# A gated cross-attention layer in f32: the down product of its feed-forward part by a 26-product scheme

## The chip, the core and the metric

The kernel runs on one core of a Trainium2 chip. A core has TensorE (PE: matrix products, out of the on-chip memory SBUF into the accumulators of PSUM), VectorE (DVE), ScalarE (ACT), GpSimd (POOL[...]) and SyncE (SP, which issues most DMA transfers). All data is f32. The metric is device time in microseconds of one execution, lower is better.

## What is computed

The input x has 64 sequences of 128 tokens with 512 features, the context ctx has the same shape. The reference, cut to what matters:

```python
x = x + tanh(g_xattn) * xattn(layernorm(x), ctx, ctx, ...)
# xattn: Q, K, V = per-head products with Wh; scores summed over the whole batch,
#        A = max(|sum_b scores * decay|, 1); O = A V; Y = norm(O) * gamma + beta
#        return (relu(x @ wg_w) * Y) @ wo_w
x = x + tanh(g_ffn) * ffn(layernorm(x), ...)
# ffn: g = (xf @ gate_w.T) * gate_s;  u = (xf @ up_w.T) * up_s
#      return ((silu(g) * u) @ down_w.T) * down_s
```

INTER, the hidden width of ffn, is 1408: 11 tiles of 128. The change concerns the last product, `(silu(g) * u) @ down_w.T`, called "down" below.

## The kernel before

The work goes in 16 groups of four sequences (512 tokens, four token tiles). A first pass over all groups normalises x, forms the scores and the gate projection, and stores what later stages need in DRAM; beside it, `prepare_weights` reads the raw weights, lets GpSimd form the sums of weight blocks that the fast schemes need, and stores them in DRAM scratch (`gu_scr`, `dn_scr`, `wo_scr`), one part per group, each part a load, its sums, and its stores one group later.

A second pass runs, for each group g, `ffn(g)`; beside it, for later groups, `attended(g+1)` (the product with wo, the residual, the second layer norm) and `next_retention(g+2)` (A V, the normalisation, the product with the gate). All three are Python generators. `interleave` draws from them in a fixed ratio: ffn has the weight FFN_STEPS, the attention chain int(23 x 1.05) = 24; the next step is drawn from the generator for which (steps done + 1) / weight is least. The order in which steps are drawn is the order of the program. From it a planner makes each engine's instruction order: by its own estimates of durations, a free engine is given, among the instructions whose operands are ready, the one that comes first in the program. An engine then runs its instructions strictly in that order, each waiting for its operands.

The big products use two-by-two schemes with seven block products in place of eight. Gate and up: `ffn` runs over five values of j; for each it takes the two INTER tiles j and 5 + j, and makes seven products of four matmuls (128x128 weights, 256 columns), each called by `product` (line 216). They accumulate in PSUM banks bank_a, bank_f, bank_b and two banks bank_c0 and bank_c1 that take turns. `hidden` (lines 783 and 784) makes silu(gate) on ScalarE and multiplies by up on VectorE. Two of the four blocks need an add out of PSUM first: c22 (line 813, out of bank_c) and c12 (line 818, out of bank_b). The order within one j is: bank_f, bank_a, bank_c (then a ScalarE copy bank_b <- bank_c, line 804), the first product of the next j into bank_a, bank_c (c22), bank_b (c12), bank_c again. The last of these waits until c22 has been read out of bank_c. After that GpSimd forms four sums of hidden blocks (lines 256 to 259, `combine_a`), the left-hand sides of down.

The eleventh INTER tile is the leftover: `rest_product` (line 850) computes it with the same scheme on half blocks, 14 matmuls in the midst of the down stage.

Down before: two halves of the tokens, two halves of INTER (five tiles each) and two halves of DIM. Each of the seven `down_product`s (line 836) has ten matmuls of 256 columns and fetches its own weights of 640 KB (line 767, three buffers); `down_rest` (line 893) adds the eleventh tile with eight matmuls. Six adds (line 902) bring 128x512 blocks out of PSUM into x_t, the residual, and two ScalarE copies (lines 880 and 913) carry a partial sum to another bank.

Beside it, VectorE does for the attention chain: the adds of the wo product (line 660), batch statistics (lines 180 and 181), normalisation (line 208) and a 32x32 block transpose (line 192) whose result goes through DRAM (`moved`, lines 198 and 201) and comes back token-transposed. In `retention` these follow for all four sequences in one step of the generator, the one after the fourth product `po` (line 571). `combine_tokens` (line 253) makes the four sums of the next group's tokens, on GpSimd after the first group; it reuses one buffer, so it starts after the last product that reads the present ones.

Of the kernel before, what the change touches and what calls it, by code (L numbers as in the profile page):

```python
# [10 lines left out]
F32 = mybir.dt.float32  # L11
# [15 lines left out]
DB11, DB21, DB22, DT1, DT2, DT3, DT4 = range(7)  # L27

# [28 lines left out]
def flamingo_gated_layer(  # L57
# [22 lines left out]
    P = 128  # L80
# [64 lines left out]
    dn_rest = const.tile([P, DIM], F32, name="dn_rest")  # L145
# [3 lines left out]
    dn_scr = dram.tile([7, P, NJ, HN], F32, name="dn_scr")  # L149
# [110 lines left out]


# [42 lines left out]
    decay = once.tile([P, H, S], F32, name="decay")  # L304
    ds = once.tile([P, DIM], F32, name="ds")
# [38 lines left out]
    def load_down(j):  # L344
        raw = once.tile([P, 2, DIM], F32, tag="raw", name="dn_raw", bufs=2)
        pair = downT[0 : REST * P].rearrange("(q j p) e -> p q j e", q=2, p=P)[:, :, j, :]
        nc.sync.dma_start(out=raw, in_=pair)
        return raw

    def sum_down(j, raw):  # L350

        for q in range(2):
            nc.gpsimd.tensor_tensor(raw[:, q], raw[:, q], ds, ALU.mult)
        t = once.tile([P, 4, HN], F32, tag="sums", name="dn_t")
        b = (raw[:, 0, 0:HN], raw[:, 0, HN:DIM], raw[:, 1, 0:HN], raw[:, 1, HN:DIM])
        combine_b(nc.gpsimd, [t[:, i] for i in range(4)], *b)
        return [
            (dn_scr[0, :, j], b[0]),
            (dn_scr[1:3, :, j].rearrange("m p e -> p m e"), raw[:, 1].rearrange("p (m e) -> p m e", m=2)),
            (dn_scr[3:7, :, j].rearrange("m p e -> p m e"), t),  # L360
        ]

    def load_down_rest():
        nc.sync.dma_start(out=dn_rest, in_=downT[REST * P : INTER])

    def sum_down_rest(_):
        nc.gpsimd.tensor_tensor(dn_rest, dn_rest, ds, ALU.mult)
        rest_weights()
        return []
# [20 lines left out]
    def prepare_weights():  # L390


        parts = [(load_wo, sum_wo)]
        for j in range(NJ):
            parts.append((partial(load_down, j), partial(sum_down, j)))
            parts.append((partial(load_gu, j), partial(sum_gu, j)))
        parts.append((load_down_rest, sum_down_rest))
        raw, stores = parts[0][0](), []
        yield
        for n, (_, sums) in enumerate(parts):  # L400
            for dst, src in stores:
                nc.sync.dma_start(out=dst, in_=src)
            stores = sums(raw)
            if n + 1 < len(parts):
                raw = parts[n + 1][0]()
            yield
        for dst, src in stores:
            nc.sync.dma_start(out=dst, in_=src)

# [27 lines left out]
    def scores(g, c_t, xnT):  # L437
# [10 lines left out]
        for h in range(H):  # L448
            if h % 2 == 0:
                tags = ("v", "sq") if g % 2 else ("ys", "yT")  # L450
                both = att.tile([P, 2, 2, 3, P], F32, tag=tags[h // 2], name="both")
# [183 lines left out]
    def attended(g, x_t, ws, x1nT):  # L635
# [4 lines left out]
        s = att.tile([P, 4, KC, HT], F32, tag="ys", name="ys")  # L640
# [97 lines left out]

    gup = ctx.enter_context(tc.tile_pool(name="gup", bufs=2))
    dnp = ctx.enter_context(tc.tile_pool(name="dnp", bufs=3))  # L740
    work = ctx.enter_context(tc.tile_pool(name="work", bufs=2))
    comb = ctx.enter_context(tc.tile_pool(name="comb", bufs=1))
    turn = [0]

# [20 lines left out]
    def down(m):  # L765
        w = dnp.tile([P, NJ, HN], F32, tag="dn", name="dn_w")
        nc.sync.dma_start(out=w, in_=dn_scr[m])
        return w

    def ffn(g, x_t, x1nT, tokens):  # L770

        b11, b21, b22, t = tokens
        h11 = comb.tile([P, NJ, HT], F32, tag="h11", name="h11")
        h21 = comb.tile([P, NJ, HT], F32, tag="h21", name="h21")
        h22 = comb.tile([P, NJ, HT], F32, tag="h22", name="h22")
        hs = comb.tile([P, 4, NJ, HT], F32, tag="hs", name="hs")
        hrest = comb.tile([P, TOK], F32, tag="hrest", name="hrest")

        def hidden(dst, src, i):

            n = dst.shape[-1]
            sil = work.tile([P, HT], F32, tag="sil", name="sil", bufs=3)
            nc.scalar.activation(sil, src[:, 0:n], AF.Silu, scale=gs_sb[:, i : i + 1])  # L783
            nc.vector.scalar_tensor_tensor(  # L784
                dst, src[:, n : 2 * n], us_sb[:, i : i + 1], sil, ALU.mult, ALU.mult
            )

        w = gu_next[0]
        product(bank_a, w[GA11], b11, True)
        yield  # L790
        for j in range(NJ):
            i1, i2 = j, NJ + j
            bank_c = next_c()
            m5 = work.tile([P, TOK], F32, tag="m5", name="m5")
            h12 = work.tile([P, HT], F32, tag="h12", name="h12")
            nc.scalar.copy(bank_c, bank_a)  # L796
            product(bank_f, w[GS1], t[:, 0], True)
            nc.scalar.copy(m5, bank_f)
            yield
            product(bank_a, w[GA12], b21, False)  # L800
            hidden(h11[:, j, :], bank_a, i1)
            yield
            product(bank_c, w[GS2], t[:, 1], False)
            nc.scalar.copy(bank_b, bank_c)  # L804
            yield
            w_j = w
            if j + 1 < NJ:
                w = gate_up(j + 1)
                product(bank_a, w[GA11], b11, True)
            yield  # L810
            product(bank_c, w_j[GS3], t[:, 2], False)
            c22 = work.tile([P, TOK], F32, tag="c", name="c22")
            nc.vector.tensor_add(c22, bank_c, m5)  # L813
            hidden(h22[:, j, :], c22, i2)
            yield
            product(bank_b, w_j[GS4], b22, False)
            c12 = work.tile([P, TOK], F32, tag="c", name="c12")
            nc.vector.tensor_add(c12, bank_b, m5)
            hidden(h12, c12, i1)
            yield  # L820
            product(bank_c, w_j[GA22], t[:, 3], False)
            hidden(h21[:, j, :], bank_c, i2)

            combine_a(
                nc.gpsimd, [hs[:, i, j, :] for i in range(4)],
                h11[:, j, :], h21[:, j, :], h12, h22[:, j, :],
            )
            yield
        if g + 1 < NG:
            gu_next[0] = gate_up(0)  # L830

        def down_product(bank, m, lhs, start):
            dn = down(m)
            for i in range(2):
                for j in range(NJ):
                    nc.tensor.matmul(  # L836
                        bank[:, i * HN : (i + 1) * HN],
                        lhsT=lhs[:, j, i * P : (i + 1) * P],
                        rhs=dn[:, j, :],
                        start=(start and i == 0 and j == 0),  # L840
                        stop=(i == 1 and j == NJ - 1),
                        skip_group_check=True,
                    )
                yield
# [10 lines left out]
        def rest_silu(gate):  # L855
            sil = work.tile([P, HT], F32, tag="sil", name="sil", bufs=3)
            nc.scalar.activation(sil, gate, AF.Silu, scale=gs_sb[:, REST:NI])
            return sil

        def rest_hidden(tok, sil, up):  # L860
            nc.vector.scalar_tensor_tensor(
                hrest[:, tok], up, us_sb[:, REST:NI], sil, ALU.mult, ALU.mult
            )

        half = slice(0, HT)
# [3 lines left out]
        nc.scalar.copy(bank_c[:, half], bank_a[:, half])  # L869
        rest_product(bank_f, GS1, t[:, 0], True)  # L870
        nc.scalar.copy(m5[:, half], bank_f[:, half])
        yield
        rest_product(bank_a, GA12, b21, False)
        sil = rest_silu(bank_a[:, half])
        rest_product(bank_c, GS2, t[:, 1], False)
        nc.scalar.copy(bank_b[:, half], bank_c[:, half])
        yield
        bank_d = next_c()
        yield from down_product(bank_f, DB11, h11, True)
        nc.scalar.copy(bank_d, bank_f)  # L880
        rest_product(bank_c, GS3, t[:, 2], False)
        c22 = work.tile([P, TOK], F32, tag="c", name="c22")
        nc.vector.tensor_add(c22[:, half], bank_c[:, half], m5[:, half])
        rest_product(bank_b, GS4, b22, False)
        c12 = work.tile([P, HT], F32, tag="h12", name="c12")
        nc.vector.tensor_add(c12, bank_b[:, half], m5[:, half])
        rest_product(bank_c, GA22, t[:, 3], False)
        rest_hidden(slice(HT, TOK), rest_silu(c12), c22[:, half])
        rest_hidden(half, sil, bank_c[:, half])
        yield  # L890
        def down_rest(bank, q, cols, stop=True):
            for i in range(2):
                nc.tensor.matmul(
                    bank[:, i * HN : (i + 1) * HN],
                    lhsT=hrest[:, (2 * q + i) * P : (2 * q + i + 1) * P],
                    rhs=dn_rest[:, cols],
                    start=False, stop=(stop and i == 1), skip_group_check=True,
                )

        def add(q, cols, bank):  # L900
            dst = x_t[q][:, :, cols]
            nc.vector.tensor_add(dst, dst, bank.rearrange("p (b d) -> p b d", b=2))
# [127 lines left out]
```

## Time and profile before

| | us |
|---|---|
| median of the runs | 2286.45 |
| the profiled execution, its own time | 2287.32 |
| its span, first to last instruction | 2285.5 |
| PE busy | 2264.5 |
| DVE busy | 901.0 |
| ACT busy | 601.4 |
| POOL busy | 670.1 |

The granted TensorE clock was 0.998 of full speed. 475.9 MB went over DMA, 208 GB/s as a mean; the queue of SP carried 457 MB of it.

A second-pass group takes 116.6 us (a product of the same place starts at 1121.10, 1237.67 and 1354.24 us). The first pass ends and the second begins near 400 us. In the stretch of gate and up of one group (1139 to 1215 us) PE was busy for 75.78 of 76 us, VectorE for 30.31, GpSimd for 20.03, and DMA 65% of the time; in the stretch of down (1215 to 1242 us) PE for all 27.00 us, VectorE 11.28, GpSimd 9.40, DMA 74%.

How to read the rows: "L836 PE MATMUL bank_f<-dn_w,h ... x640 | 143.5, 379" is the line of the kernel, the engine, the operation, what is written from what, the shapes, the number of records, their busy time in us and the mean of one in ns; what follows the second bar is the engine's idle time ahead of them and what ended it. A row of the timeline starts with the start and the duration in us; "x8" are eight records of one group in a row, and a bracket at its end is the idle time ahead of it and its releaser. One f32 matmul of the code leaves two records.

### The profile page before, as it was taken

The numbers are of one execution on the slowest core, as the hardware profiler recorded it, in microseconds if no ns is written. First come the engines' busy times: TensorE is split into PE (matmuls) and PEld (weight loads), VectorE is DVE, ScalarE is ACT, GpSimd is POOL, SyncE is SP. The second block draws the span as 40 slices with busy tenths as digits, with TensorE's granted clock in tenths as the row PEclk, the third lists the DMA queues.
The fourth block names the chain that finished last, engine by engine and source line by source line (L and its number), as shares of the span: only waits on it lengthen the run. The fifth ranks groups of instructions, "written<-read, shape, count | busy, mean of one in ns | idle before, by whom it ended". The sixth has DMA issues, their size and how long they took to land.

```text
span 2285.5 us, 27188 instructions
## 1 busy us (share of the span) xinstructions
PE 2264.5 (99%) x10304; PEld 1925.1 (84%) x10304; DVE 901.0 (39%) x1835; ACT 601.4 (26%) x1116; POOL 670.1 (29%) x811
## 2 busy tenths in 40 slices
PE   8999999999999999999999999999999999999999
PEld 6878887778888888888888888888888888888888
DVE  6544443654434343434343434333434333333222
ACT  3444444321212122212122222222221212121221
POOL 4222300232242424233323242424232323333210
PEclk9999999999999999999999999999999999999999
DMA  8787875766666665656565756666666656564541
GB/s 279 251 275 259 266 246 164 257 209 218 206 209 212 208 213 196 214 197 219 185 223 187 226 191 220 188 223 191 221 200 207 214 191 219 199 203 159 166 150 65
DMA packets 167794, 475.89 MB, mean 208 GB/s; under 512 B 16112, under 2 KB 52592, under 8 KB 150896
## 3 DMA queue, kind: packets, MB, share of 16 engines
q1 hardware_dynamic: 162240, 457.12, 61.2%
q10 hardware_dynamic: 5424, 17.04, 1.9%
q8 instruction: 81, 1.33, 0.2%
q14 instruction: 49, 0.40, 0.1%
HBM read 376.72 MB, written 97.39 MB: 207 GB/s over the span
## 4 chain that ended last, share of the span: by engine, by line
PE 93%; DVE 3%; DMA 1%; POOL 1%; issue 1%; SPq 0%; ACT 0%; ACTq 0%; DVEq 0%; POOLq 0%
PE bank_c L216 20%; PE bank_a L216 13%; PE bank_c L836 9%; PE bank_f L216 7%; PE bank_f L836 6%; PE bank_b L216 6%; PE sv L457 4%; PE by L649 3%; PE bank_b L836 3%; PE bank_a L836 3%; PE bz L649 2%; PE bx L649 2%; PE pq L442 2%; PE po L571 2%; PE bank_c L850 2%; PE bank_a L850 1%
## 5 line engine op out<-in xcount | busy, mean ns | idle before, releaser
L216 PE MATMUL bank_c<-tcomb,gu 128*128 128x256 f32 x1920 | 456.3, 380 | 3.7 <-DVE c L813 3.0
L216 PEld LDWEIGHTS bank_c<-tcomb,gu 128*128 128x128 f32 x1920 | 362.2, 190 | 72.2 <-ACT bank_b L804 10.1
L216 PE MATMUL bank_a<-x1nT,gu 128*128 128x256 f32 x1280 | 303.0, 379 | 0.7 <-ACT bank_c L796 0.7
L216 PEld LDWEIGHTS bank_a<-x1nT,gu 128*128 128x128 f32 x1280 | 242.8, 190 | 40.4 <-issue 6.2
L256 POOL TENSOR_TENSOR hs<-h,h 128x256 f32<-128x256 f32 x80 | 58.1, 727 | 649.8 <-DVE h L784 649.8
L176 POOL TENSOR_TENSOR rs<-ve,mhalf 128x1 f32<-128x1 f32 x128 | 73.5, 586 | 318.9 <-DVE ve L175 303.7
L783 ACT ACTIVATE sil<-c,gs_sb 128x256 f32<-128x256 f32 x160 | 81.2, 508 | 285.3 <-DVE c L813 184.8
L216 PE MATMUL bank_b<-x1nT,gu 128*128 128x256 f32 x640 | 151.6, 379 | 0.0
L216 PE MATMUL bank_f<-tcomb,gu 128*128 128x256 f32 x640 | 151.3, 379 | 0.0
L836 PE MATMUL bank_c<-dn_w,hs 128*128 128x256 f32 x640 | 145.0, 382 | 0.0
L813 DVE TENSOR_TENSOR c<-bank_c,m 128x512 f32<-128x512 f32 x80 | 54.7, 684 | 227.1 <-PE bank_c L216 223.7
L836 PE MATMUL bank_f<-dn_w,h 128*128 128x256 f32 x640 | 143.5, 379 | 0.0
L836 PEld LDWEIGHTS bank_c<-dn_w,hs 128*128 128x128 f32 x640 | 120.3, 190 | 19.8 <-ACT bank_b L913 4.0
L836 PEld LDWEIGHTS bank_f<-dn_w,h 128*128 128x128 f32 x640 | 121.6, 190 | 17.4 <-issue 1.0
L216 PEld LDWEIGHTS bank_b<-x1nT,gu 128*128 128x128 f32 x640 | 121.9, 190 | 16.7
L216 PEld LDWEIGHTS bank_f<-tcomb,gu 128*128 128x128 f32 x640 | 121.6, 190 | 16.5
L630 POOL TENSOR_TENSOR w_t<-w_t,yT 128x256 f32<-128x256 f32 x112 | 77.9, 727 | 159.7 <-ACT yT L621 159.7
L180 DVE BATCH_NORM_STATS2 st<-x_t 128x6 f32<-128x512 f32 x128 | 83.8, 682 | 94.0 <-DMA x_t<-in_x_dram 92.9
L457 PE MATMUL sv<-qw,c_t 128*128 128x256 f32 x512 | 120.4, 379 | 0.0
L784 DVE SCALAR_TENSOR_TENSOR h<-c,us_sb,sil 128x256 f32<-128x256 f32 x160 | 78.5, 491 | 84.3 <-ACT sil L783 84.3
L783 ACT ACTIVATE sil<-bank_a,gs_sb 128x256 f32<-128x256 f32 x80 | 37.9, 474 | 277.1 <-PE bank_a L216 277.1
L660 POOL TENSOR_TENSOR x_t<-x_t,m 128x512 f32<-128x512 f32 x48 | 60.8, 1296 | 168.3 <-ACT m L666 168.3
(166 smaller groups left out, 3484.4 us busy)
## 6 DMA issues: line engine op xcount, KB each, us to landing
gu<-gu_scr SPq DMA_DIRECT2D x80, 1024.0 KB, 4.9
dn_w<-dn_scr SPq DMA_DIRECT2D x112, 640.0 KB, 4.0
gu<-gu_scr SPq DMA_DIRECT2D x80, 768.0 KB, 4.8
x_t<-in_x_dram SPq DMA_DIRECT2D x62, 512.0 KB, 5.5
sq_scr<-sq SPq DMA_DIRECT2D x30, 1024.0 KB, 4.2
wo_w<-wo_scr SPq DMA_DIRECT2D x112, 256.0 KB, 2.7
c_t<-in_ctxT_dram SPq DMA_DIRECT2D x64, 256.0 KB, 4.9
v_scr<-both SPq DMA_DIRECT2D x32, 512.0 KB, 6.5
```

Of the source, the lines that this page charges most:

```text
L176: nc.gpsimd.tensor_tensor(dst, ve, mhalf[:, :n], ALU.pow)
L180: nc.vector.bn_stats(st, src)
L216: nc.tensor.matmul(out, lhsT=w[:, s, k, :], rhs=x_k, start=(start and s == 0 and k == 0), stop=(s == 1 and k == KC - 1), skip_group_check= ...
L256: engine.tensor_tensor(s[0], a21, a22, ALU.add)
L457: nc.tensor.matmul(sv[:, 0 : 2 + i : 1 + i, :], lhsT=c_t[j][:, h, :], rhs=qw[:, h, j : GB + 1 : GB - j, :], start=(i == 0), stop=(i == 1), ...
L630: (helper if d else nc.gpsimd).tensor_tensor(w, w, yT[:, :, d * KC + k, q * 2 : q * 2 + 2, :], ALU.mult)
L649: nc.tensor.matmul(bank[:, i * HN : (i + 1) * HN], lhsT=lhs[:, k, i * P : (i + 1) * P], rhs=w[:, k, :], start=(start and i == 0 and k == 0 ...
L660: engine.tensor_tensor(dst, dst, src.rearrange("p (b d) -> p b d", b=2), ALU.add)
L783: nc.scalar.activation(sil, src[:, 0:n], AF.Silu, scale=gs_sb[:, i : i + 1])
L784: nc.vector.scalar_tensor_tensor(dst, src[:, n : 2 * n], us_sb[:, i : i + 1], sil, ALU.mult, ALU.mult)
L836: nc.tensor.matmul(bank[:, i * HN : (i + 1) * HN], lhsT=lhs[:, j, i * P : (i + 1) * P], rhs=dn[:, j, :], start=(start and i == 0 and j == ...
L850: nc.tensor.matmul(out, lhsT=gu_rest[:, m, k, :], rhs=x_k, start=(start and k == 0), stop=(k == KC - 1), skip_group_check=True,)
```

## The change

Down becomes a scheme for four token tiles, four tiles of INTER and two halves of DIM: 26 products of 128x128 by 128x256 in place of 32. The eleven INTER tiles are dealt out as DOWN_QUADS: two quads (0, 1, 6, 5) and (2, 3, 8, 7), each with 26 products, and a triple (10, 9, 4), with which 20 of the 26 suffice. The quads and the triple share the order DOWN_STEPS: 24 steps, each with an accumulator, one or two products, each with up to three matmuls (one of either quad, one of the triple), and the blocks of x_t to which the accumulator is added or from which it is subtracted. An accumulator is not cleared between its steps: each add reads the running sum in place, and the signs in DOWN_STEPS are chosen for that. There are six accumulators of 256 columns: a, f, b0, b1, c0, c1, in five banks.

- The left-hand sides are sums of 128x128 hidden tiles, made in place in 26, 26 and 20 slots: 28 sums for each quad (H_SUMS), 18 for the triple (H_SUMS3). The first quad's are on GpSimd (18 at j = 2, 10 at j = 3), eight of the second's too (j = 3); its other 20 are on VectorE at j = 4. The triple's are on VectorE: eight after c12 of j = 4, ten after the last product.
- VectorE clears bank_b, half of bank_c1 and half of bank_c0 by memsets ahead of down.
- The leftover tile's gate and up products go first in the group.
- The first five steps ("roots") run with both quads first, then with the triple.
- The weights of one product are a tile of 128 x 3 x 256, two thirds of it where the triple is left out; nine buffers, the first nine fetched during gate and up, each further one after the product that frees its buffer.
- 28 adds of 128x256 go into x_t, in place of six of 128x512; the two copies are gone.
- In the preparation, the weight sums of down are made per quad: 8 products with the scale (three of them on VectorE) and 18 sums of 128x256 for a quad, 6 and 12 for the triple. `prepare_weights` takes all gate/up parts first, then the three of down.
- FFN_STEPS is 50 (it was 56). `both` takes turns in three buffers in place of four, `ys` shares the buffer of `sq`, `decay` and `ds` live in buffers of wo.

```diff
-    def down(m):
-        w = dnp.tile([P, NJ, HN], F32, tag="dn", name="dn_w")
-        nc.sync.dma_start(out=w, in_=dn_scr[m])
+    def down(n):
+        w = dnp.tile([P, 3, HN], F32, tag="dn", name="dn_w")
+        tiles = 3 if in_three[n] else 2
+        nc.sync.dma_start(out=w[:, 0:tiles], in_=dn_scr[weights_at[n], :, 0:tiles])
         return w
...
+        sums = {
+            2: [(nc.gpsimd, 0, H_SUMS[:18])],
+            3: [(nc.gpsimd, 0, H_SUMS[18:]), (nc.gpsimd, 1, H_SUMS[:H_EARLY])],
+            4: [(nc.vector, 1, H_SUMS[H_EARLY:])],
+        }
...
             product(bank_b, w_j[GS4], b22, False)
             c12 = work.tile([P, TOK], F32, tag="c", name="c12")
             nc.vector.tensor_add(c12, bank_b, m5)
-            hidden(h12, c12, i1)
+            hidden(i1, 1, c12[:, lo], c12[:, hi])
+            some_sums()
+            if j == NJ - 1:
+                nc.vector.memset(bank_b, 0.0)
+                nc.vector.memset(bank_c1[:, 0:HN], 0.0)
+                sum_tiles(nc.vector, h_slots[2], H_SUMS3[:H_EARLY3])
...
+        nc.vector.memset(bank_c0[:, 0:HN], 0.0)
+        sum_tiles(nc.vector, h_slots[2], H_SUMS3[H_EARLY3:])
...
+        def down_product(acc, n, a, q, start):
+            nc.tensor.matmul(
+                places[acc], lhsT=hq[q][:, a, :], rhs=dn[n][:, q, :],
+                start=start, stop=True, skip_group_check=True,
+            )
+
+        def down_steps(n_steps, quads):
+            for i in n_steps:
+                acc, products, to = steps[i]
+                for n, a, a3 in products:
+                    for q in quads:
+                        if q < 2 or a3 is not None:
+                            first = i < DOWN_ROOTS and q == 0 and acc in "af"
+                            down_product(acc, n, a if q < 2 else a3, q, first)
+                    if 2 in quads and len(dn) < len(weights_at):
+                        dn.append(down(len(dn)))
+                if 2 not in quads:
+                    continue
+                for block, sign in to:
+                    b, d = block // 2, block % 2
+                    dst = x_t[b // 2][:, b % 2, d * HN : (d + 1) * HN]
+                    nc.vector.tensor_tensor(
+                        dst, dst, places[acc], ALU.add if sign > 0 else ALU.subtract
+                    )
...
+        down_steps(range(0, 3), (0, 1))
+        yield
+        down_steps(range(3, DOWN_ROOTS), (0, 1))
+        yield
+        down_steps(range(0, DOWN_ROOTS), (2,))
+        yield
+        for i in range(DOWN_ROOTS, len(steps), 2):
+            down_steps(range(i, min(i + 2, len(steps))), (0, 1, 2))
+            yield
 
     gu_next = [gate_up(0)]
-    FFN_STEPS = 1 + 7 * NJ + 3 + 17
+    FFN_STEPS = 2 + 7 * NJ + 3 + (len(DOWN_STEPS) - DOWN_ROOTS + 1) // 2
```

`sum_tiles(engine, slots, sums)` makes one `tensor_tensor` (add or subtract) for each entry (to, a, b, sign).

## The prediction

> **What bounds the kernel now.** I read the page's busy times first, then the groups by shape, then the timeline of one steady group of four sequences (the one that starts its down products at 1215 us), engine by engine.
>
> ```profile
> PE 2264.5 (99%) x10304; PEld 1925.1 (84%) x10304; DVE 901.0 (39%) x1835; ACT 601.4 (26%) x1116; POOL 670.1 (29%) x811
> ...
> PE 93%; DVE 3%; DMA 1%; POOL 1%; issue 1%; SPq 0%; ACT 0%; ACTq 0%; DVEq 0%; POOLq 0%
> ```
>
> TensorE carries 93% of the chain that ended last; the other engines have room on average. So a removed matmul is worth its full place in PE's stream, and any new wait of PE costs its full length. What one matmul costs is not its mean duration:
>
> ```profile
> L836 PE MATMUL bank_f<-dn_w,h 128*128 128x256 f32 x640 | 143.5, 379 | 0.0
> ```
>
> ```profile
> 1215.69 4.48 PE L836 MATMUL bank_f<-dn_w,h 128*128 128x256 f32 x20
> ```
>
> Each f32 matmul of the code is two records (a down product has 2 x 5 matmuls and shows x20). Twenty records take 4.48 us from the first start to the last end, of which the last takes 0.379: (4.48 - 0.379)/19 = 0.216 us from start to start. A matmul of 256 columns is 0.43 us of PE, an eight-record product 1.73 us.
>
> **What is removed.** Down of one group is now 7 x 10 + 8 = 78 matmuls; after it is 26 + 26 + 20 = 72 (DOWN_STEPS has 26 products, six of which leave out the triple). 6 matmuls x 2 records x 16 groups = 192 records x 0.216 = 41.4 us. By the mean of 379 ns it would be 73 us, but those durations overlap. [...] The row decides: 41.4 us, or 2.59 us per group. Two ScalarE copies (bank_f and bank_c, 0.57 each) go too; they lie beside PE and count nothing.
>
> **What is added, per group.**
>
> ```profile
> L253 DVE TENSOR_TENSOR tcomb<-x1nT 128x512 f32<-128x512 f32 x2 | 1.3, 680 | 0.0
> ...
> L630 DVE TENSOR_TENSOR w_t<-w_t,yT 128x256 f32<-128x256 f32 x8 | 2.8, 419 | 0.0
> ...
> L945 DVE TENSOR_TENSOR x_t<-x_t,bank_c 128x256 f32<-128x256 f32 x2 | 0.8, 421 | 4.8 <-PE bank_c L940 4.8
> ...
> L256 POOL TENSOR_TENSOR hs<-h,h 128x256 f32<-128x256 f32 x80 | 58.1, 727 | 649.8 <-DVE h L784 649.8
> ```
>
> ```profile
> 467.33 1.43 DVE L630 TENSOR_TENSOR w_t<-w_t,yT 128x256 f32<-128x256 f32 x4
> ```
>
> The sums of hidden tiles are 128x128, a shape the trace lacks. From 680 and 419 ns a DVE element costs 1.02 ns, so 419 - 131 = 0.29 us alone; four in a row start (1.43 - 0.419)/3 = 0.34 us apart, so 0.21 us in a row. VectorE gets 38 of them (20 + 18): 8.0 to 11 us. It gets 28 adds of 128x256 out of PSUM (0.34 to 0.42: 9.5 to 11.8 us) in place of six of 0.69, and three PSUM memsets. No row shows such a memset: between 0.145 (a 128x1 operation, L175) and 0.69 (a 128x512 copy, L575); I take 0.45 for the full bank and 0.3 for a half. In sum 15 to 20 us more per group of 113 us: VectorE goes from 39% to about 54%. GpSimd gets 36 sums of 128x128 (727 and 1267 ns for 256 and 512 elements give 0.46) for 20 of 0.73: 16.5 for 14.5 us. All this would fit beside PE, were it spread. It is not: most sits between the last gate/up products and the first down products.
>
> **Where VectorE becomes late.** The planner gives a free engine the ready instruction that comes first in the program:
>
> ```profile
> 1180.63 1.89 PE L216 MATMUL bank_c<-tcomb,gu 128*128 128x256 f32 x8
> ...
> 1183.12 0.70 DVE L192 STREAM_TRANSPOSE sq<-xn 128x512 f32<-128x512 f32 x1
> 1183.75 0.65 DVE L813 TENSOR_TENSOR c<-bank_c,m 128x512 f32<-128x512 f32 x1
> ...
> 1184.46 1.99 PE L216 MATMUL bank_c<-tcomb,gu 128*128 128x256 f32 x8 [0.21 <-DVE c L813]
> ...
> 1214.89 1.29 DVE L180 BATCH_NORM_STATS2 st<-o 128x6 f32<-128x512 f32 x2
> ...
> 1221.38 0.42 DVE L883 TENSOR_TENSOR c<-bank_c,m 128x256 f32<-128x256 f32 x1
> ```
>
> The add of line 813 had its bank at 1182.5 and started at 1183.75, behind attention work emitted before it; PE's next product into that bank waited. The second pair shows retention's normalisation: 6.5 us without a gap in which later-emitted work could enter, about 8.0 us in all. Today it is emitted after ffn step 39 of 57, beside a down product that asks nothing of VectorE. With 50 steps in place of 56 in the interleave's weights, and the leftover products moved ahead, the same count (step 17 of 24) puts it after ffn step 35, inside the last gate/up tile (j = 4), ahead of c22, c12, the memsets and the last sums.
>
> From the end of retention's fourth product (t = 0) VectorE has, in program order: copy of o 0.6, the block 8.0, c22 0.6, hidden 0.4, c12 0.6, hidden 0.4, two memsets 0.75, eight early sums of the triple 1.7, hidden 0.4, memset 0.3, ten late sums 2.2 (a few follow their own operand). With 0.2 to start: 16.2 us, and only then the first down add, done at 16.6. PE has four products (6.9) and the 15 matmuls of the five roots (6.5): 13.4 us, after which step 5 needs the bank that this add frees. I grant that PE fills its waits inside this stretch with roots a and f, ready early. Then 16.7 - 13.4 = 3.3 us of PE wait remain. Queued behind that wait are all later down steps; after it the adds (28 x 0.34 = 9.5 us) keep up with 57 matmuls (24.6 us), as five accumulators leave four steps (about 4 us) for one add.
>
> [...] When the last product of j = 4 ends, the four GpSimd sums of the next group's tokens (tcomb, 1.27 each) may start; the 18 sums of the triple run then.
>
> ```profile
> 468.48 4.47 POOL L660 TENSOR_TENSOR x_t<-x_t,m 128x512 f32<-128x512 f32 x3 [1.80 <-ACT m L666]
> 468.67 1.49 DVE L784 SCALAR_TENSOR_TENSOR h<-c,us_sb,sil 128x256 f32<-128x256 f32 x1
> 470.08 1.75 DVE L256 TENSOR_TENSOR ys<-w_t 128x512 f32<-128x512 f32 x1
> ...
> 1223.91 0.73 DVE L861 SCALAR_TENSOR_TENSOR hrest<-c,us_sb,sil 128x256 f32<-128x256 f32 x1
> ```
>
> Beside a run of GpSimd operations, VectorE operations with both inputs in SBUF took 1.49 and 1.75 us for 0.48 and 0.69: 1.0 us more each, one per GpSimd operation. Line 861 beside tcomb took 0.73 for 0.45, 0.28 more. [...] By line 861 four waits are 1.1 us. [...]
>
> **Other parts.** Weights: 72 tiles of 131 KB are 9.4 MB per group for 4.6. Nine tiles (3.4 MB) are fetched during gate/up, where the trace by stretches has DMA 65% busy, the rest beside down (74%); I cost it at nothing, covered by nine tiles ahead (7 us or more against a median landing of 4.0); uncovered, see below. Preparation: 61 GpSimd operations of 0.73 (44 us) for about 29, three bursts of 11 to 17 us in groups of 24.6, and 4.85 MB more of stores (about 16 us of DMA at 300 GB/s) where DMA is 70 to 89% busy; SP's loads of x and ctx queue behind the stores. 0 to 20 us; I take 5, as GpSimd was idle most of the time there. Leftover first: the same 14 matmuls, each ScalarE copy (0.36 + 0.26 to start) under a 0.86 us product: nothing, up to 0.3 us per group. Fewer buffers for "both" and ys sharing sq: each earlier reader is over a group stage before: nothing.
>
> **The sum.** Groups 1 to 13: 3.3 + 3.3 - 2.6 = +4.0 us each; group 0, whose block falls just ahead of the late sums, the same; groups 14 and 15 have no block: -2.6 each. 14 x 4.0 - 5.2 + 5 = +56 us on the profiled execution's 2287.3 (span 2285.5), which is 0.9 above the median: 2343 us.
>
> **Rivals.**
> - *The whole gain* (25%): the planner slips c22 and the sums into retention's block, or VectorE's pipelining makes it shorter by 3 us, and PE never waits. For it: VectorE is 39% busy and the old trace has 0.2 us of such waits per group. Against: the order of lines 192 and 813 above. 2287 - 41 + 5 = 2250; it decides once VectorE's stretch is under 13.4 us instead of 16.2.
> - *Wait without the port* (11%): 3.3 or, with line 861's price, 4.4 us per group: +0.7 to +1.8 x 14 = 2297 to 2312.
> - *Weights late* (10%): 17 refills beside down, SP held 4.5 us behind retention's store and gather (sq issued at 1223.65, its read at 1228.15): 7 - 4.5 - 4 = 1.5 us late per group, 24 us on top of the gain: 2275; on top of my case 2367.
> - That fewer products do not appear (1%) would show at once in the records.
>
> My case has 53%, with its own range 2312 to 2390: below, the port at 1.1 us; above, four full waits, sums at 0.29 and preparation at 20. The range over cases is 2250 to 2390: the better half of the whole gain (about 12%) and a little of late weights lie outside. A measurement of this kernel tells about 2% (46 us) from no change; the most that can be gained is 41.4 plus odd idle, so faster has 0.04. Slower (over 2332) has seven tenths of my case and most of late weights: 0.45. The rest, 0.51, is same.
>
> **What would show it.** Down records 144 per group for 156; PE waiting for DVE at the first down steps and at the j = 4 product into bank_c0, 5 to 7 us per group, groups 14 and 15 shorter by 2 us or more; VectorE sums of 128x128 near 0.2 to 0.3 us but over 1 us beside tcomb. I am wrong if c22 of j = 4 runs within 1 us of its bank, or if PE waits for dn_w.

## The result and the profile after

The changed kernel takes 2386.59 us (median of four runs, 2383.83 to 2387.89) against 2286.45 for the kernel before, measured beside it (2284.39 to 2287.91; one further run of it, of 7297.9 us, is not counted): a ratio of 1.0437, 95% interval 1.0417 to 1.0458. The forecast was 2343, so the sign and the range held and the size was 44 us short. The profiled execution has a span of 2382.0 us (2285.5 before), at a granted clock of 0.986 (0.998 before).

From the page of the kernel after, the busy time, share and records of each engine, and the shares of the chain that ended last by engine:

```profile
PE 2261.5 (95%) x10112; PEld 1905.3 (80%) x10112; DVE 1196.7 (50%) x2851; ACT 584.5 (25%) x1084; POOL 717.8 (30%) x1097
...
PE 78%; DMA 11%; DVE 6%; POOL 2%; issue 1%; SPq 1%; ACT 1%; ACTq 0%; DVEq 0%; POOLq 0%
```

The 192 records are gone (10304 to 10112), but PE's busy time fell by 3.0 us only, not by 41.4, and its idle time grew from 21.0 to 120.5 us. In the chain PE has 78% for 93%, DMA 11% for 1%; the two largest DMA shares there are the store `sq_scr<-sq` (5%) and the gather `yT<-sq_scr` (4%) of the retention's normalisation. The forecast had spoken of VectorE alone. TensorE's waits, in total, times, longest:

```profile
PE bx L728 <- POOL w_t L709: 37.0, 16, 3.9
PE bank_c L1000 <- DVE bank_c L980: 33.1, 14, 2.4
PE bank_b L1000 <- DVE bank_b L969: 18.3, 13, 1.4
PE bank_c L1000 <- DVE ve L244: 6.3, 1, 6.3
```

The second and third are the memsets of the accumulators, late as forecast; the fourth is the same junction in group 0. The first is not in the forecast: bx is the first wo product of the next group, and w_t needs the gathered yT, on ScalarE and then GpSimd. TensorE in the down stage of one steady group:

```profile
1260.42 1.89 PE L285 MATMUL bank_c<-tcomb,gu 128*128 128x256 f32 x8
...
1272.79 1.56 PE L1000 MATMUL bank_b<-dn_w,h 128*128 128x256 f32 x6 [1.41 <-DVE bank_b L969]
1276.75 1.13 PE L1000 MATMUL bank_c<-dn_w,h 128*128 128x256 f32 x4 [2.40 <-DVE bank_c L980]
...
1279.08 1.56 PE L1000 MATMUL bank_c<-dn_w,h 128*128 128x256 f32 x6 [0.33 <-DVE x_t L1020]
...
1288.89 0.70 PE L728 MATMUL bx<-wo_w,w_t 128*128 128x256 f32 x2 [2.21 <-POOL w_t L709]
1289.43 2.47 PE L1000 MATMUL bank_a<-dn_w,h 128*128 128x256 f32 x6
1291.69 2.17 PE L1000 MATMUL bank_f<-dn_w,h 128*128 128x256 f32 x6
```

The product behind retention's fourth starts at 1260.42, the run of step 5 (`bank_c`, x6) at 1279.08, 18.7 us later; without waits it would be the forecast's 13.4, so the junction costs 5.3 us here (6.6 in the forecast). Then the planner has put bx between two down steps, PE waits 2.2 us for it, and the two runs of six records behind it take 2.47 and 2.17 us in place of 1.46 (by the prediction's 0.216 us per record). Of these same times, by stretch of 4 us (span, busy time and records of PE, PEld, DVE, ACT and POOL, then granted clock, DMA share, GB/s):

```profile
1270.00:1274.00 4.00, 2.59 (x13) 1.93 (x11) 3.90 (x6) 0.47 (x1) 3.40 (x3) 1.00 0.57 141
1274.00:1278.00 4.00, 1.60 (x8) 1.12 (x7) 3.95 (x13) 0.00 (x0) 1.94 (x2) 1.00 0.94 344
...
1282.00:1286.00 4.00, 4.00 (x20) 3.54 (x19) 1.81 (x5) 0.00 (x0) 0.00 (x0) 1.00 1.05 224
1286.00:1290.00 4.00, 1.79 (x9) 1.20 (x8) 0.59 (x2) 2.78 (x4) 1.89 (x3) 0.97 1.02 372
1290.00:1294.00 4.00, 4.00 (x13) 3.27 (x12) 0.52 (x2) 0.15 (x1) 3.92 (x6) 0.61 1.04 397
```

In this group the wait shows twice: as 2.2 us of idle time, and in a granted clock of 0.61 over the 4 us after it. Over the whole trace, the runs of 256-column matmuls last 44.1 us longer than 0.216 us per record explains; before it was 10.9. So 33 of the 41.4 us that the removed records were worth are lost again to slower matmuls; another 5 us of busy time came on top, whose cause is open. What holds bx up is seen in SP's queue:

```profile
1270.55 0.32 SPq L843 DMA_DIRECT2D gu<-gu_scr  x1
1270.96 0.38 SPq L267 DMA_DIRECT2D sq_scr<-sq  x1
1271.44 1.51 SPq L851 DMA_DIRECT2D dn_w<-dn_scr  x2
1279.56 1.74 SPq L270 DMA_DIRECT2D yT<-sq_scr  x4
1281.40 12.81 SPq L851 DMA_DIRECT2D dn_w<-dn_scr  x11
```

The gather (yT) is issued 8.6 us after its store (sq), SP stands still for 6.6 us of them, and the refills of down weights stand behind it in the queue. In a group of the kernel before it was 4.5 us:

```profile
1223.65 0.32 SPq L198 DMA_DIRECT2D sq_scr<-sq  x1
...
1228.15 2.23 SPq L201 DMA_DIRECT2D yT<-sq_scr  x4
```

All over the trace SP waited, for the store ahead of a gather (of yT or of x1nT), in total, times, longest, after and before:

```profile
SPq L270 <- DMA sq_scr<-sq: 176.5, 29, 7.8
...
SPq L201 <- DMA sq_scr<-sq: 48.9, 21, 4.4
```

A group takes about 123 us (116.6 before). Group 14, the first with no retention beside it (groups count from 0), takes 111.7; retention's own products are 3.4 us of the difference.

### The profile page after: what moved, and what is told of

It reads as the page before. It is cut to its first block, busy times and chain, and to the rows that moved or that the text cites. A ratio compares the mean times of both kernels' runs of the same rounds, so it can differ in the third digit from the quotient of the medians.

```text
span 2382.0 us, 28908 instructions
## 1 busy us (share of the span) xinstructions
PE 2261.5 (95%) x10112; PEld 1905.3 (80%) x10112; DVE 1196.7 (50%) x2851; ACT 584.5 (25%) x1084; POOL 717.8 (30%) x1097
## 4 chain that ended last, share of the span: by engine, by line
PE 78%; DMA 11%; DVE 6%; POOL 2%; issue 1%; SPq 1%; ACT 1%; ACTq 0%; DVEq 0%; POOLq 0%
PE bank_c L285 18%; PE bank_a L285 13%; PE bank_f L285 7%; PE bank_b L285 6%; DMA sq_scr<-sq 5%; PE bank_b L1000 4%; PE bank_c L1000 4%; PE sv L536 4%; DMA yT<-sq_scr 4%; PE by L728 3%; PE bx L728 3%; PE bank_a L1000 2%; PE bz L728 2%; PE bank_f L1000 2%; DVE st L249 2%; PE bank_c L884 2%
## 5 line engine op out<-in xcount | busy, mean ns | idle before, releaser
L333 POOL TENSOR_TENSOR h<-h 128x128 f32<-128x128 f32 x576 | 251.3, 466 | 354.1 <-DVE h L874 350.3
L1000 PE MATMUL bank_c<-dn_w,h 128*128 128x256 f32 x896 | 224.4, 390 | 42.4 <-DVE bank_c L980 33.1
L1000 PEld LDWEIGHTS bank_c<-dn_w,h 128*128 128x128 f32 x896 | 172.5, 195 | 76.1 <-DVE bank_c L980 38.8
L873 ACT ACTIVATE sil<-c,gs_sb 128x256 f32<-128x256 f32 x176 | 89.4, 508 | 378.1 <-DVE c L957 230.5
L1000 PE MATMUL bank_b<-dn_w,h 128*128 128x256 f32 x640 | 155.7, 381 | 18.7 <-DVE bank_b L969 18.3
L333 DVE TENSOR_TENSOR h<-h 128x128 f32<-128x128 f32 x608 | 170.7, 341 | 3.7 <-DVE h L874 0.5
L1000 PEld LDWEIGHTS bank_b<-dn_w,h 128*128 128x128 f32 x640 | 120.6, 190 | 40.3 <-DVE bank_b L969 23.5
L739 POOL TENSOR_TENSOR x_t<-x_t,m 128x512 f32<-128x512 f32 x48 | 60.7, 1292 | 301.1 <-ACT m L745 301.1
L874 DVE SCALAR_TENSOR_TENSOR h<-c,us_sb,sil 128x256 f32<-128x256 f32 x176 | 97.7, 555 | 66.6 <-ACT sil L873 66.6
L874 DVE SCALAR_TENSOR_TENSOR h<-bank_a,us_sb,sil 128x256 f32<-128x256 f32 x80 | 38.4, 480 | 168.7 <-ACT sil L873 168.6
```

The costliest lines, as they stand in the source:

```text
L333: engine.tensor_tensor(slots[to], slots[a], slots[b], ALU.add if sign == "+" else ALU.subtract)
L739: engine.tensor_tensor(dst, dst, src.rearrange("p (b d) -> p b d", b=2), ALU.add)
L873: nc.scalar.activation(sil, gate, AF.Silu, scale=gs_sb[:, i : i + 1])
L874: nc.vector.scalar_tensor_tensor(hidden_at(i, tok), up, us_sb[:, i : i + 1], sil, ALU.mult, ALU.mult)
L1000: nc.tensor.matmul(places[acc], lhsT=hq[q][:, a, :], rhs=dn[n][:, q, :], start=start, stop=True, skip_group_check=True,)
```

## The experiments

Three things could be late: the memsets on VectorE (junction), the gathered yT with its bx, and the weights behind the gather. The trace shows the first two. All times below stand against a kernel before of 2285.0 to 2286.5 us, run beside them. The last column is what TensorE waited for most.

| run | dn_w buffers | block | token sums | bx | us | TensorE's waits, us |
|---|---|---|---|---|---|---|
| after | 9 | in j=4 | GpSimd | free | 2386.6 | bx 37.0, memsets 51.4 |
| e1 | 9 | in j=4 | GpSimd | held | 2374.0 | dn_w 26.2, memsets 51.4 |
| e2 | 9 | in j=4 | VectorE | free | 2388.1 | bx 81.5, memset 5.0 |
| e3 | 9 | 3 later | GpSimd | free | 2365.8 | bx 41.7, x_t and memset 32.4 |
| e4 | 9 | 3 later | VectorE | held | 2307.6 | dn_w 31.9 |
| e7 | 9, refills by ScalarE | 3 later | VectorE | held | 2296.2 | dn_w 17.8, copies 10.2, bx 8.1 |
| e8 | 11 | in j=4 | GpSimd | free | 2333.6 | memsets 51.4, bx 2.7 |
| e9 | 11 | 3 later | GpSimd | free | 2302.7 | x_t and memset 32.5, ScalarE's m 14.8 |
| e10 | 11 | in j=4 | VectorE | free | 2354.8 | bx 52.0, memset 5.0 |
| e12 | 10 | in j=4 | VectorE | held | 2366.6 | dn_w 55.7, memset 5.0 |
| e11 | 10 | 3 later | VectorE | held | 2263.1 | ScalarE's m 14.8 |
| e6 | 11 | 3 later | VectorE | held | 2260.7 | ScalarE's m 14.8 |

### One limit at a time

**e1**: bx kept behind the last down matmul.

```diff
-        wo_product(bx, DB11, a11, True)
+        if last_down[0] is None:
+            wo_product(bx, DB11, a11, True)
+        else:
+            with tc.issue_after(last_down[0].ins):
+                wo_product(bx, DB11, a11, True)
...
-            nc.tensor.matmul(
+            last_down[0] = nc.tensor.matmul(
```

> The first matmul of the next group's wo product (bx) is kept behind the last down matmul; nothing else is changed. Theory A (PE waits for w_t in the middle of down only because the planner put this one matmul there, and the slow clock after it is a result of that wait): 2.3 us of wait and about 1.8 us of slow matmuls go in 15 groups, so 2387 - 60 = 2325 to 2335 us, and no wait for w_t or dn_w is left in that place. Theory B (the weights of down step 11 are late as well, since their transfers queue behind the gather of retention): PE waits about as long at the same step, now for dn_w, and the time stays at 2370 to 2390 us. The waits for the memsets (1.4 and 2.4 us per group) stay in both.

Measured 2374.04, ratio 1.039 (1.0374 to 1.0405). The wait for w_t is gone and another has its place:

```profile
PE bank_c L1005 <- DVE bank_c L985: 33.1, 14, 2.4
PE bank_a L1005 <- DMA dn_w<-dn_scr: 26.2, 14, 2.8
```

The weights of the next step were late as well. The trace of after could not show it, because bx stood in front of that step and waited as long. Theory B is right in its mechanism and its range.

**e2**: the token sums of the later groups on VectorE.

```diff
-        pending = (g + 1, x_t, x1nT, combine_tokens(nc.gpsimd, x1nT))
+        pending = (g + 1, x_t, x1nT, combine_tokens(nc.vector, x1nT))
```

> The four token sums of the next group go to VectorE in place of GpSimd; nothing else is changed. [...] Theory B (VectorE has simply too much to do there): 2.4 us more on VectorE make it 2385 to 2410 us.

Measured 2388.09, ratio 1.045 (1.0428 to 1.0473), within 2 us of the changed kernel:

```profile
PE bx L728 <- POOL w_t L709: 81.5, 16, 6.5
PE bank_b L1000 <- DVE bank_b L969: 5.0, 13, 0.4
```

The memset waits fall from 51.4 to 5.0 us, so GpSimd's sums beside VectorE's do make them late; but nearly all of it comes back at bx (81.5 for 37.0), and the time is in theory B's range, though not for B's reason. The traces fit a w_t whose time does not depend on PE: who comes to it earlier waits longer.

**e3**: retention's normalisation block emitted three steps of the generator later.

```diff
+        if g > 1:
+            for _ in range(LATER):
+                yield
...
-        for _ in range(WAIT):
+        for _ in range(WAIT - LATER if g > 1 else WAIT):
             yield
...
-    WAIT = 5
+    WAIT, LATER = 5, 3
```

> Retention's normalisation is emitted three generator steps later, behind the roots of down in place of ahead of c22 of j = 4, with three waiting steps fewer after it; nothing else is changed. Theory A (this block, being first in program order, holds VectorE): c22 runs within 0.7 us of its bank, the waits for both memsets (3.8 us per group) are gone, a wait of 0 to 2 us for adds comes in the first steps after the roots; 2387 - 14 x 2 to 3.8 = 2334 to 2359 us. Theory B (the sums alone fill VectorE): the memset waits stay above 2 us per group and the time within 10 us of 2387.

Measured 2365.75, ratio 1.0353 (1.0333 to 1.0374): 21 us less, between the ranges of the two theories: the waits for the memset fell to 11.2 us, but x_t is waited for (21.2), and bx still is (41.7).

**e4**: the three edits together.

> The three edits together: bx behind the last down matmul, token sums on VectorE, normalisation three steps later. Theory A (these three are what the change lost): the 41 us of fewer matmuls come through, less 7 us in the first pass and 1 to 2 us of remaining waits per group: 2255 to 2285 us, faster than or equal to the kernel before. Theory B (late weights or the load on DMA bound the down stage): 2310 us or more, with PE waiting for dn_w.

Measured 2307.62, ratio 1.0099 (1.0077 to 1.012). One by one the edits gave 12.6, -1.5 and 20.8 us, 32 in sum; together 79. So the limits are not terms of a sum: of several late things the latest sets the time. Theory A is missed by 23 us; what is left is the weights, as in theory B:

```profile
PE bank_f L1008 <- DMA dn_w<-dn_scr: 31.9, 13, 3.0
```

### The block's place in the kernel before

**e5** is the kernel before with a lower weight of ffn in the interleaving, so that the block falls inside j = 4 as it does after the change.

```diff
-    FFN_STEPS = 1 + 7 * NJ + 3 + 17
+    FFN_STEPS = 1 + 7 * NJ + 3 + 10
```

> The kernel of before; only the weight of the feed-forward part in the interleaving is lowered (29 for 36 at the end of its count), so that the retention's normalisation block is emitted inside pass j=4, ahead of c22, c12, the memsets and the sums, as in the changed kernel. Theory A (the block's place on VectorE is a cost of its own, 3.3 us a group in 14 groups): 2320 to 2335, with TensorE waiting for VectorE at the last pass or the first down steps. [...]

Measured 2275.65, ratio 0.9956 (0.9941 to 0.997): it is 10 us faster, where theory A had it slower. Why it is faster stays open. The place of the block is no cost by itself. In the kernel before, neither the memsets and the sums stand behind it on VectorE nor a row of small refills behind its store on SP; that this is the reason was argued, not tried.

### The stock of weights

**e6**: e4 with 11 buffers of down weights; **e8**: the 11 buffers alone.

```diff
-    AHEAD = 9
+    AHEAD = 11
...
-            sil = work.tile([P, HT], F32, tag="sil", name="sil", bufs=3)
+            sil = work.tile([P, HT], F32, tag="sil", name="sil", bufs=2)
```

> The changed kernel with all three edits (bx held, token sums on VectorE, block later) and 11 buffers of down weights for 9 (the SiLU tile has 2 buffers for 3, to make room). With the three edits alone: 2307.6 us, of which TensorE waits 33 us for dn_w, up to 3.0 us a group, and runs some 13 us at a lower clock after it. Two more tiles are 2.6 us of TensorE time, so the late tile should be nearly hidden. Theory A (weights are the last limit): 2262 to 2280, wait for dn_w under 8 us, faster than the kernel before. Theory B (another wait behind it, such as bx or x_t, takes its place): 2295 to 2310.

> The changed kernel with 11 buffers of down weights for 9 (SiLU tile 2 for 3) and nothing else. Theory A (limits in series: VectorE's junction sets the start of the down steps, then w_t for bx, and the weights are late only behind those): 2375 to 2388, waits for w_t and the memsets as they were. Theory B (the weights alone are the loss): 2340 to 2355.

e6 takes 2260.74 us, ratio 0.9896 (0.9882 to 0.9911), 1% faster than the kernel before and just better than theory A's range; against e5, the kernel before with its block early, it is 15 us. e8 takes 2333.61, ratio 1.0214 (1.0199 to 1.0229): the stock alone is worth 53 us, more than each theory had expected of it, and theory A of that run falls: the weights do not come in only behind the other two. Not all of the 53 us is the weights' own, though: holding bx alone gave 12.6 (e1), and bx hardly waits in e8, so about 40 us (e1 to e8) are what the stock gives once bx is out of the way. TensorE's waits in e8:

```profile
PE bank_c L1000 <- DVE bank_c L980: 33.1, 14, 2.4
PE bank_b L1000 <- DVE bank_b L969: 18.3, 13, 1.4
...
PE bx L728 <- POOL w_t L709: 2.7, 5, 1.1
```

The junction is as it was; the wait for bx is gone, though nothing was done to it. In e8 the planner has placed bx two down runs later, behind the ones into bank_a and bank_f. So bx wanted w_t 13.5 us after the product that waits for the last memset, where in after it was 9.9 us, and w_t came after 12 to 13 us in both. The planner goes by its own estimates; that it advanced bx because it took the weights of those runs to be late is likely, but was not shown.

**e11** is e4 with 10 buffers and the SiLU tile unchanged.

> The changed kernel with all three edits and 10 buffers of down weights, the SiLU tile with its 3 buffers: 9 gave 2307.6 us, 11 with 2 SiLU buffers 2260.7. One tile more is 1.3 us of TensorE time against a wait of up to 3.0 us. If the stock's depth sets the loss: 2276 to 2290, with half of the wait for dn_w left. If 11 gained by something else (its SiLU tile, its order): 2300 to 2310; if one tile is enough: 2255 to 2265.

Measured 2263.11, ratio 0.9904 (0.9887 to 0.992): one tile is enough, and what e6 gained was the stock, not the SiLU tile.

**e7**: e4 with the refills on ScalarE's queue.

```diff
-        nc.sync.dma_start(out=w[:, 0:tiles], in_=dn_scr[weights_at[n], :, 0:tiles])
+        queue = nc.scalar if n >= AHEAD else nc.sync
+        queue.dma_start(out=w[:, 0:tiles], in_=dn_scr[weights_at[n], :, 0:tiles])
```

> The changed kernel with all three edits, 9 buffers, and the refills of down weights (the tiles from the tenth on) issued on ScalarE's queue instead of SyncE's, so that they don't stand behind the retention's gather, which waits for its store. Theory Q (the place in the queue makes them late, 2.5 us a group): wait for dn_w under 10 us, 2265 to 2285. Theory W (the 16 DMA engines are full there, the gather's small packets slow everything): the wait stays at 20 to 33 us, 2295 to 2310.

Measured 2296.15, ratio 1.0043 (1.0028 to 1.0059). The wait for dn_w went from 33 to 18 us, between the theories, the time is at theory W's lower end, and others came up: bank_a for a ScalarE copy 10.2, bx 8.1. The place in the queue is a part of the lateness. For the rest, the 16 DMA engines being full (in the changed kernel a share of 1.02 to 1.05 from 1282 to 1294 us, while the refills come in) would be an explanation; it was not isolated.

### What the junction is made of

With 11 buffers the junction alone is left (e8), so its two halves can be told apart there.

**e9**: e8 with the block later. **e10**: e8 with the token sums on VectorE.

> The changed kernel with 11 buffers of down weights (2333.6 us alone) and the retention's normalisation block emitted three steps later. What is left of the loss there is TensorE's waits for the two memsets, 51 us, and about 20 us of lower clock beside them. Theory A (the block's place makes the memsets late, as predicted 3.3 us a group): 2275 to 2300. [...]

> [...]

e9: 2302.74, ratio 1.0077 (1.0062 to 1.0092), 31 us less, 3 us above theory A's range. From e9 to e6 the token sums go to VectorE and bx is held; bx waited only 1.5 us in e9 as in e6, while 32.5 us of waits for x_t and the memset go, so the 42 us between them are put down to GpSimd's token sums beside VectorE: 3.0 us in each of 14 groups. e10: 2354.8, ratio 1.0302 (1.0286 to 1.0318), 21 us more than e8. As in e2, the memset waits vanish (5.0) and bx waits, 52.0 us in place of 2.7:

```profile
1271.37 1.46 PE L1000 MATMUL bank_f<-dn_w,h 128*128 128x256 f32 x6
1276.55 1.22 PE L728 MATMUL bx<-wo_w,w_t 128*128 128x256 f32 x2 [3.72 <-POOL w_t L709]
1277.56 3.38 PE L1000 MATMUL bank_b<-dn_w,h 128*128 128x256 f32 x10
```

Bx has the same place as in e8. TensorE arrives earlier, waits 3.7 us, and the ten records behind it take 3.38 us for 2.32. Taking 46 us of waits at the junction away gave 49 us of waits at bx, and the matmul runs grew longer by 44.1 us for 33.0 in e8.

**e12** was to settle it: 10 buffers, token sums on VectorE, bx held, the block left in j = 4.

> The changed kernel with 10 buffers of down weights, the token sums on VectorE and bx held behind the last down product; the normalisation block stays inside pass j=4, where the change puts it. With the block three steps later this is 2263.1 us; with 11 buffers and bx not held 2354.8 us. [...] Theory A (the block's place costs TensorE 2 to 3.3 us a group by itself): 2290 to 2312. Theory G (what stands in e10 is a late gather, which holding bx only turns into another wait): 2310 to 2345.

Measured 2366.63, ratio 1.0354 (1.0337 to 1.0371). I had held that the block's place costs nothing once the token sums are off GpSimd; this falls by 100 us, as only the block's place sets e12 apart from e11 (2263.1). Theory G has the mechanism, and set its price too low: with bx held, TensorE waits for weights. TensorE in one group of e12:

```profile
1272.65 2.75 PE L1005 MATMUL bank_c<-dn_w,h 128*128 128x256 f32 x12
1275.24 1.46 PE L1005 MATMUL bank_a<-dn_w,h 128*128 128x256 f32 x6
1280.71 2.90 PE L1005 MATMUL bank_f<-dn_w,h 128*128 128x256 f32 x6 [4.01 <-DMA dn_w<-dn_scr]
1283.40 2.52 PE L1005 MATMUL bank_b<-dn_w,h 128*128 128x256 f32 x10
```

SP's queue in the same group of e12:

```profile
1262.96 0.40 SPq L268 DMA_DIRECT2D sq_scr<-sq  x1
1263.45 1.41 SPq L856 DMA_DIRECT2D dn_w<-dn_scr  x2
1271.69 1.74 SPq L271 DMA_DIRECT2D yT<-sq_scr  x4
1273.54 6.62 SPq L856 DMA_DIRECT2D dn_w<-dn_scr  x8
```

And in a group of e11, where the same run of twelve records starts at 1225.13:

```profile
1218.85 4.64 SPq L859 DMA_DIRECT2D dn_w<-dn_scr  x7
1225.40 0.32 SPq L268 DMA_DIRECT2D sq_scr<-sq  x1
1225.82 1.34 SPq L859 DMA_DIRECT2D dn_w<-dn_scr  x2
1230.84 1.74 SPq L271 DMA_DIRECT2D yT<-sq_scr  x4
1232.69 6.22 SPq L859 DMA_DIRECT2D dn_w<-dn_scr  x8
```

In e11 seven weight loads go out ahead of the store, from 6.3 us before that run. In e12 the store and the wait for it stand in front: SP issues two loads and then nothing until 1271.69, and the refills start 0.9 us after the run began. The block's early place is paid in SP's queue, over 4 us a group, and in slower matmuls (47.3 us of longer runs over the trace, 10.6 in e11). How much of the lateness is the order in the queue and how much the load on the 16 DMA engines is no more separated here than in e7.

## Why the prediction was right in its sign and short in size

**The sum.** The forecast had 92 us of waits at the junction (14 x 6.6), 41.4 gained, 5 for the preparation, and nothing else: +56. By the trace, PE's idle time grew by 99.5 us: 60.7 are waits at the junction (33.1, 18.3, 6.3 and 3.0 for x_t), 37.0 are waits for bx. Its busy time fell by 3.0: 41.4 less for the records, 33 more for slower runs, and the 5 whose cause is open. So the junction was priced too high and two terms were missing; that the total came within the range is in part luck.

**What is removed: right.** The 192 records are gone, 144 are left in each group's down, and where nothing is late PE's busy time falls by what was worked out: e6 has 2222.1 us, 42.4 under the kernel before, for 41.4.

**What is added: right.** VectorE has 295.7 us more, 18.5 per group (forecast 15 to 20), and is busy 50% of the span (forecast 54). The memsets take 0.48 and 0.27 us (0.45 and 0.3 taken), GpSimd's sums 0.466 (0.46). VectorE's sums, by group of the changed kernel:

```profile
L333 DVE TENSOR_TENSOR h<-h 128x128 f32<-128x128 f32 x608 | 170.7, 341 | 3.7 <-DVE h L874 0.5 <-issue 0.3
```

The mean of 341 ns mixes two prices, seen in the timeline of the same group as above:

```profile
1272.65 2.24 DVE L333 TENSOR_TENSOR h<-h 128x128 f32<-128x128 f32 x3
...
1276.61 2.08 DVE L333 TENSOR_TENSOR h<-h 128x128 f32<-128x128 f32 x10
```

Three sums beside GpSimd's tcomb took 2.24 us, ten without it 2.08. GpSimd, and the multiplication that ran beside its first sums:

```profile
1270.60 2.67 POOL L322 TENSOR_TENSOR tcomb<-x1nT 128x512 f32<-128x512 f32 x2 [1.44 <-PE bank_c L285]
1273.23 2.78 POOL L322 TENSOR_TENSOR tcomb<-x1nT,tcomb 128x512 f32<-128x512 f32 x2
...
1270.68 1.47 DVE L874 SCALAR_TENSOR_TENSOR h<-c,us_sb,sil 128x256 f32<-128x256 f32 x1
```

**VectorE beside GpSimd's token sums: the size right, the working not shown.** In the traced group the multiplication beside tcomb took 1.0 us longer (1.47 for 0.48), three sums 1.6 and two 0.7: 3.3 us. With the other limits away, e9 and e6 differ by 3.0 us a group, where four times line 861's 0.28 would be 1.1. The forecast's sum has a second 3.3 us a group for this, and its rivals call it the port: no run shows that term as it was worked out, nor any port; what the runs show in its place are these longer operations, and memset waits of 5.0 us for 51.4 once the sums are off GpSimd (e2, e10).

**VectorE's junction: the mechanism right, the size too high, the reason incomplete.** 3.3 us a group were put on the block ahead of the memsets. Moving the block with the stock deep gave 2.2 (e8 to e9). Together with the token sums the junction is 73 us (e8 to e6), 5.2 a group for 6.6. In e8, where it is nearly the only limit, the kernel takes 2333.6 us; the forecast for that case was 2343. The nearness is in part luck: the memset waits of e8 are 51.4 us, 3.7 a group, and the rest is mostly the slower matmuls (33.0 us for 10.9 before), which the forecast did not have. And the working treated the block's place as a matter of VectorE's order. e5 shows that the place costs nothing there without the change's other work, and e12 that it can cost more through SP's queue than through VectorE.

**Weights and gather: the step that failed.** "I cost it at nothing, covered by nine tiles ahead (7 us or more against a median landing of 4.0)". The landing time was taken from a kernel with other transfers, and it is counted from the issue, which is what was late: the refills stood behind a gather issued 8.6 us after its store (4.5 in the forecast's rival "weights late", the row of before). The stores themselves landed later, 7.1 us in the median for 4.2, and the weights too, 5.2 us for 4.0 (the tiles of two thirds 6.4). The stock lasts only while PE works through it. The same late gather held up bx, a wait that no case of the forecast had: in the changed kernel it is what shows, 37.0 us, and with bx out of the way the weights show, 26.2 us (e1). The rival gave 1.5 us a group, 24 us, 2367 on top of the forecast's case; two more tiles take 53 us away, about 40 of them by the weights (e8). So the rival was priced at about half, and its chance of 10% was too low.

**What would show it: too narrow.** "If PE waits for dn_w" was named as a sign against the forecast, and the trace shows no such wait. It was there all the same, one step behind the wait for bx (e1). The sign that c22 of j = 4 would be late was right: its bank was ready 2.85 us before it ran.

```profile
1263.01 1.95 PE L285 MATMUL bank_c<-tcomb,gu 128*128 128x256 f32 x8
...
1267.81 0.66 DVE L957 TENSOR_TENSOR c<-bank_c,m 128x512 f32<-128x512 f32 x1
```

At 1267.81 it stands inside the block, not behind all of it: the block's last normalisation and transpose come later (1269.19 and 1270.05), so the planner slipped it in sooner than the working had it.

**The clock: not in the sum.** Each wait was priced by its length. The 33 us of longer matmuls are a third of the 100 us between the kernels.

**Preparation and leftover: right; the last groups in part.** The first retention product starts 6.6 us later than before (400.5 for 393.9; 5 taken). The leftover's new place shows no wait of its own but one of 1.6 us, in group 0. Groups 14 and 15 were to be shorter than before by 2 us or more. From the first product of j = 4 of group 14 to that of group 15 it is 100.1 us (2237.17 to 2337.25) for 100.3 before (2130.91 to 2231.24), as a memset was waited for once more, 2.0 us. From there to the end of the span it is 44.8 us for 54.3, of which 6.0 are the leftover's 14 matmuls, now ahead: 3.5 us shorter.

With these limits moved away, the scheme is worth 25 us on the kernel before (e6), not the 37 of the rival "the whole gain": the preparation takes 6.6 us where the rival had 5, and in e6 PE waits 14.8 us for ScalarE's copies `m`.

## What to carry to other kernels

A wait hides the waits behind it: PE stands in one place at a time, so the list of waits names the first of several late things, and taking one away shows the next. Before a change shortens the engine that is the bound, follow every queue that feeds it and ask what stands in front of each refill, above all a transfer that waits for another's landing; the time from issue to landing says nothing of the time before the issue. Try suspects together as well as alone: three edits worth 32 us one by one were worth 79 together, and one of them was worth nothing or less until the others were made.

## What the runs showed of the hardware

The granted clock fell after some short waits and not after others. In the changed kernel it was 1.00 from 1270 to 1278 us, although PE had been busy for only 4.2 of these 8 us, with idles of 1.4 and 2.4 us; with the idle of 2.2 us ahead of bx it was 0.97 from 1286 to 1290 us and 0.61 in the next 4 us. So here an idle of 2.2 us was followed by a fall, and one of 2.4 us, 12 us earlier, was not. The other groups show the same: of thirteen waits of 2.4 us for a memset, four were followed by a slow run (four records in 2.07 us), nine were not (1.13 us). So the length of the idle alone does not tell.

Every GpSimd instruction of the two traces (811 before, 1097 after) had its operands in SBUF; more than that no run shows of what GpSimd can reach.
